# One layout change in a DRAM scratch copy: x stored by whole rows instead of by quarter rows

## The chip, the cores and the metric

The kernel runs on one core of one Trainium2 chip. The metric is the device time of one execution in microseconds (us). The kernel before was timed three times; the median is 4287.6 us. A further execution was profiled, and every view of the profile below is of that one.

## The reference, cut to what matters

The input x is 32 images of 48 channels, 64 rows (h) and 128 columns (w), in fp32: 50.3 MB. Two layers follow each other. Each layer normalises its input by groups of channels (the mean and the variance over 3 channels, 64 rows and 128 columns), sends the result through four scans, and adds the layer's unnormalised input back, which the texts below call the residual.

```python
def step(w, b):
    def f(carry, inp):
        nxt = inp + _conv1d(carry, w, b)     # 48 -> 48 channels, 5 taps
        return (nxt, nxt)
    return f
# down over h, up over h, right over w, left over w: 63, 63, 127, 127 steps
x = x + conv(_gn(x), layer 0)
x = x + conv(_gn(x), layer 1)
```

Every step of a scan needs the whole result of the step before. So the 2 x 4 scans form a long chain of small convolutions, and batches of images are the only thing that is independent.

## The kernel before, in words

**Tiles.** The images are taken in 4 groups of 8 (`GB`). A position along h or w is split into a block and a place within the block, each block 8 long (`E8`): w = 8k + e, with 16 blocks k; h = 8a + i, with 8 blocks a. One row of one group fills 3 tiles (`NG`) of 128 partitions, which hold 8 places e x 48 channels (the list `PIECES` says which partitions hold which), by 128 elements, which are 16 blocks k x 8 images b. One step of a scan (`step`, L728) is 9 products of 128x128 on TensorE (L741) into 3 PSUM tiles, and 3 additions on VectorE (L750), which write the new row or column in place. The column scans use the same tiles with the roles of h and w exchanged.

**Phases.** Twelve phases follow each other (`PHASES`). They are named by their number k from 0: 0 rows of group 0 in layer 0; 1 rows of group 1; 2 columns of groups 0 and 1 together; 3 rows of group 2; 4 rows of group 0 in layer 1; 5 rows of group 3 (layer 0); 6 columns of groups 2 and 3 in layer 0; 7, 8, 9 rows of groups 1, 2, 3 in layer 1; 10 and 11 the columns of layer 1. A row phase has 126 steps, a column phase 254. The names of the PSUM tiles in the profile carry this: `step_11d` is layer 1, group 1, scan down, so phase 7; `step_01l` is layer 0, pair 1, scan left, so the end of phase 6.

**Data between phases.** Three arrays in DRAM carry it. `xin` (`source[0]`) holds x in the order of the tiles, `ups` (`upa`, `upb`) the result of the row phases, and `mid` (`source[1]`) the input of layer 1.

- x is read in its own order (`take_in`, L553), permuted in SBUF by `permute` (L560, copies at L569) and written to `xin` by `put_out` (L571). `permute` makes four copies for a row r, one for each quarter q of 4 blocks k. Each copy writes 256 elements in one contiguous run (the order is e, k, b) and reads them with the image innermost, so with a step of 8 KB in the first group and 2 KB later. One call treats row h = r of the upper half of the image and h = 32 + r of the lower half, on 96 partitions (48 channels x 2 halves).
- The order of `xin` before, `mid` and `ups` is, for each channel: i, q, a, e, then 32 elements (4 blocks k x 8 images). A row read (`by_row`, used by `move_rows`, L589) so meets runs of 32 elements, 128 bytes. A column read (`by_col`) for one quarter q meets a x e x 32 elements in one run, 8 KB.
- `move_rows` moves rows between DRAM and the slots in SBUF, in pieces of 8 rows and 10 DMAs. All go to SP's queue.
- `load_residual` (L663) reads the residual of one unit (128 partitions x 2048 elements, 1 MB; a column phase has 24 units, 4 quarters j x 6) from `source[layer]` by `by_col`. In layer 0 it goes to SP's queue, in layer 1 to ACT's. `add_residual` (L670, on GpSimd, at L673) adds it, and `keep_result` (L675) writes the unit to `mid`, on SP's queue.

**What sets the order of the work.** The function `in_order` chains what each engine and each queue gets in the order of an agenda; `at(t, fn, ...)` puts a piece of work on the agenda at step number t of the scans. So SP's queue is one fixed list of DMAs. In a column phase with the left scan from step `left`, unit u is added at about left + 34 + 32 per quarter + 4.5 per unit; four staging tiles hold the residuals, and the load of unit u is issued 3 steps after the addition of unit u - 4. The rows of the following row phase (`plan_rows`, L853) are read 16 at a time at 28 and 12 steps before the phase starts, and 4 and 20 steps after it, and scaled by ACT (`scale_rows`, L606, the ACTIVATEs at L614) 13 steps before and 3, 19, 35 steps after. The steps are positions in the lists: an engine or queue that is late delays all that stands behind.

**The first group** (`first_group`, L1024) has its own list, since nothing covers it. x of group 0 is read in two halves of 16 + 16 rows r; VectorE takes its statistics (L422); rows h = 0 to 7 come straight from products with a 0/1 matrix (L1074); the others are permuted, put out to `xin`, and read back 8 rows at a time by `move_rows`, and scaled. Permuted rows pass through a ring of spare SBUF areas (`free`, `late`, `later`), so an area is written again only after its put-out has landed.

Of the kernel before, what the change touches and what calls it, by code (L numbers as in the profile page):

```python
# [42 lines left out]
GB = 8  # L43
E8 = 8
FULL = 128
NG = E8 * C // FULL
NQ = 4
# [73 lines left out]
def kernel(  # L121
# [8 lines left out]
    nc = tc.nc  # L130
    B, _, H, W = x.shape
    NK = W // E8
    NH = H // E8
    KQ = NK // NQ
    WQ = W // NQ
    N = NK * GB
    RUN = KQ * GB
    LINE = E8 * RUN
# [75 lines left out]
    def by_row(t, e, h0, h1):  # L214


        t = t.rearrange("c (i q a e n) -> e a c i q n", i=E8, q=NQ, a=NH, e=E8)[e, h0 // E8]
        return t[:, h0 % E8 : h0 % E8 + h1 - h0].rearrange("c i q n -> c (i q) n")

    def lines(t, h0, h1):  # L220

        t = t.rearrange("c (i q a n) -> a c i q n", i=E8, q=NQ, a=NH)[h0 // E8]
        return t[:, h0 % E8 : h0 % E8 + h1 - h0].rearrange("c i q n -> c (i q) n")

    def by_col(t, e, j):


        return t.rearrange("c (i q n) -> i q c n", i=E8, q=NQ)[e, j]

    def dma(dst, src, queue=None):  # L230
        (queue or nc.sync).dma_start(dst, src)
# [21 lines left out]
    def pieces(o):  # L253
        return [(e, c0, c1, p0) for e, c0, c1, g, p0 in PIECES if g == o]
# [22 lines left out]
    def sided(t):  # L277

        return t.rearrange("(c s) n -> s c n", s=2)
# [280 lines left out]
    def permute(nat, r0, perm, engines):  # L560

        rows = perm.shape[-1] // (W * GB)
        src = nat.rearrange("p b (r q k e) -> p r q e k b", q=NQ, k=KQ, e=E8)
        dst = perm.rearrange("p (r q e k b) -> p r q e k b", r=rows, q=NQ, e=E8, b=GB)
        for i in range(rows * NQ):
            r, q = divmod(i, NQ)
            eng = engines[i * len(engines) // (rows * NQ)]
            copy = eng.copy if eng is nc.scalar else eng.tensor_copy
            copy(dst[:, r, q], src[:, r0 + r, q])  # L569

    def put_out(g, r, perm):  # L571


        n = perm.shape[-1] // (W * GB)
        for s in range(2):
            h = s * HALF + r
            dma(
                lines(source[0][g], h, h + n),
                sided(perm)[s].rearrange("p (m n) -> p m n", n=LINE),
            )  # L580


    def row_views(k):
        return [slot[i].rearrange("p (o h n) -> p o h n", o=NG, h=HALF) for i in slots(k)]
# [4 lines left out]
    def move_rows(k, h0, h1, to_dram):  # L589

        _, layer, g = PHASES[k]
        view = row_views(k)[h0 // HALF]
        t = (ups if to_dram else source)[layer][g]
        for h in range(h0, h1, E8):
            end = min(h1, h + E8)
            for o in range(NG):
                for e, c0, c1, p0 in pieces(o):
                    here = view[p0 : p0 + c1 - c0, o, h % HALF : h % HALF + end - h]
                    here = here.rearrange("p h (q n) -> p (h q) n", q=NQ)
                    there = by_row(t, e, h, end)[c0:c1]  # L600
                    if to_dram:
                        dma(there, here)
                    else:
                        dma(here, there)
# [58 lines left out]
    def load_residual(k, j, i, nat):  # L663
        _, layer, pair = PHASES[k]
        o, half = UNITS[i]
        t = source[layer][2 * pair + half]
        for e, c0, c1, p0 in pieces(o):
            dma(nat[p0 : p0 + c1 - c0], by_col(t, e, j)[c0:c1], nc.scalar if layer else None)

    def add_residual(k, j, i, nat, eng=nc.gpsimd):  # L670
        o, half = UNITS[i]
# [161 lines left out]
    def plan_input(g, times, work, lag, nats, perms):  # L833

        stats = InputStats(f"x{g}", 0)
        rows = nats[0].shape[-1] // W
        ahead, pieces_of = len(nats), rows * W // BN
        per = rows * W * GB // perms[0].shape[-1]
        for j, t in enumerate(times):
            nat = nats[j % ahead]  # L840
            if j == 0 and g > 1:
                at(t - 7, take_in, g, 0, nat)
            for i in range(per):
                perm, r = perms[i % len(perms)], i * rows // per
                at(t + i * work / per, permute, nat, r, perm, [nc.gpsimd])
                at(t + i * work / per + 4, put_out, g, rows * j + r, perm)
            at(t + lag, stats.take_others, pieces_of * j, nat)
            if j + ahead < len(times):
                free = t + 7
                at(free, take_in, g, rows * (j + ahead), nat)  # L850
        spread(t + work + lag + (0, 2, 32, 5)[g], scaling(f"x{g}", 0, g, stats, x_masks, (0, 0, 8, 0)[g]), 1)

    def plan_rows(k, t0, prev):  # L853
        if k == 1:
            ahead, scaled = (-34, -18, -3, 12), (-12, -2, 17, 33)
        elif prev == "cols":
            ahead, scaled = (-28, -12, 4, 20), (-13, 3, 19, 35)
        else:
            ahead, scaled = (-54, -43, 0, 11), (-22, -8, 16, 30)
        if k:  # L860
            for i in range(4):
                at(t0 + ahead[i], move_rows, k, i * LOAD, (i + 1) * LOAD, False)
                at(t0 + scaled[i], scale_rows, k, i * LOAD, (i + 1) * LOAD)

        cuts = list(range(0, H + 1, E8))
        following = PHASES[k + 1][0] == "cols"
        if following and follows(k + 1):
            cuts = [0, E8 // 4] + cuts[1:]
        for h0, h1 in zip(cuts, cuts[1:]):
            t = t0 + 2 * (H - 1) - h0  # L870
            if k == 0:
                t += 16 if h0 >= HALF else 68
            elif not following:
                t = t0 + 92 + 5 * (H - h1) / E8 + (34 if h1 <= HALF else 0)
            at(t, move_rows, k, h0, h1, True)
        at(
            t0 + H - 1,
            nc.gpsimd.tensor_copy,
            last.rearrange("p (o n) -> p o n", o=NG),
            row(k, H - 1),  # L880
        )
# [6 lines left out]
    def plan_cols(k, t0, prev):  # L888
# [46 lines left out]
        for u, (t, j, i) in enumerate(direct):  # L935
            nat = tiles[u % n]
            o, half = UNITS[i]
            if u < n:
                at(left + 16, load_residual, k, j, i, nat)
            if layer == 0:  # L940
                if u >= n:
                    at(direct[u - n][0] + 3, load_residual, k, j, i, nat)
                at(t, add_residual, k, j, i, nat)
                at(t + 4, keep_result, k, j, i)
                unit = quarter(k, j)[:, half, o]
                if half == 0:
                    for b in range(GB):
                        at(t + 5 + b, stats[0].take, j, o, unit, b)
                else:
                    at(t + 1, stats[1].take, j, o, unit)  # L950
            else:

                at(t, add_residual, k, j, i, nat)
                at(t + 2.5, permute_unit, k, j, i, nat, (nc.gpsimd, nc.scalar, nc.scalar))
                if final or j not in HELD:
                    at(t + 4.5, store_result, k, j, i, nat)
                else:
                    at(t + 4.5, hold_result, j, i, nat)
                if final and j == 1:
                    at(t + 4.7, load_residual, k, 0, i, last_tiles(k)[i])  # L960

                if u >= 2 and u - 2 + n < len(direct):
                    at(t + 4.6, load_residual, k, *direct[u - 2 + n][1:], tiles[(u - 2) % n])
# [60 lines left out]
    def first_group():  # L1024
# [35 lines left out]
        def permute_rows(i, r0, r1, ring, *engines):  # L1060
            for r in range(r0, r1):
                permute(parts[i], r, ring[r % len(ring)], engines)

        def put_rows(i, r0, r1, ring):
            for r in range(r0, r1):
                put_out(0, i * rows + r, ring[r % len(ring)])
# [38 lines left out]
        for b in range(GB):  # L1105
            stats.take(NBN // 2, parts[1], b)
            stats.aggregate(b)
        move_rows(0, 8, 16, False)
        for r in range(0, 8, 2):
            permute_rows(1, r, r + 2, free, nc.gpsimd)  # L1110
# [98 lines left out]
```

## Time and profile before

| | us |
|---|---|
| three timed runs | 4284.73, 4287.6, 4297.19 |
| median | 4287.6 |
| profiled execution | 4290.3 |
| its span in the profile | 4288.2 |
| TensorE products busy in the span | 4058.9 |
| first step of phase 0 starts at | 107.8 |
| phase 3 starts, ends | 1167.3, 1427.1 |
| phase 7 starts, ends | 2442.1, 2705.3 |
| last step ends | 4207.7 |

The page gives busy time by engine, busy tenths in 40 slices (107.2 us each), the DMA queues and the costliest groups of instructions. Further views come from the same trace: stretches of time with the busy time of each engine in each (with the granted TensorE clock, the busy share of the 16 DMA engines and GB/s), timelines of one engine or queue, and lists of who waited for whom. In a group's line, `arena<-xin` means that the tile `arena` is written from `xin`. `arena` and `early` are the two large SBUF tiles, which hold the slots, the staging tiles and the spare areas. A row scan without a wait takes 124.4 us for its 63 steps (from 1679.9 to 1804.2 in the first scan of phase 5), so 1.97 us a step.

### The profile page before, as it was taken

What the parts mean: (1) busy time and instruction counts of PE and PEld (TensorE: products, weight loads), DVE (VectorE), ACT (ScalarE), POOL (GpSimd) and SP (SyncE); (2) the same over time, 40 slices, a digit from 0 to 9 for tenths busy, and PEclk for the clock granted to TensorE, in tenths of its full rate; (3) what the DMA queues carried; (4) which work ended last, traced back from release to release, by engine and by line L of the source; (5) the groups of instructions that cost most, each with busy time, mean ns of one, the idle gap of its engine ahead of it and who ended that gap; (6) DMA issues with size and microseconds to landing.
All of it is one profiled execution on the core that took longest, in us unless ns stands there. A gap on an engine that the chain in (4) does not pass through costs nothing. (4 is left out here: it accounts for less than half of the span.)

```text
span 4288.2 us, 89979 instructions
## 1 busy us (share of the span) xinstructions
PE 4058.9 (95%) x36648; PEld 4029.3 (94%) x36648; DVE 2164.5 (50%) x6503; ACT 1340.1 (31%) x2662; POOL 886.2 (21%) x906
## 2 busy tenths in 40 slices
PE   3699998999999999998999999999999999999992
PEld 1699998999999999998999999999999999999992
DVE  6345444446664444444446654444444444444443
ACT  1584301435793564100006772613000002210122
POOL 4271001325323020010005310000000024510352
PEclk9899999999999999999999999999999999999996
DMA  9599799857998979679308979939289049999999
GB/s 213 113 216 162 105 167 168 245 127 213 230 198 156 163 140 160 103 127 206 85 1 242 222 154 149 148 50 161 43 140 200 1 78 247 247 243 156 180 202 182
DMA packets 2116733, 680.12 MB, mean 159 GB/s; under 512 B 2005440, under 2 KB 2056160, under 8 KB 2076384
## 3 DMA queue, kind: packets, MB, share of 16 engines
q1 hardware_dynamic: 2015904, 581.64, 70.2%
q10 hardware_dynamic: 97216, 86.44, 9.9%
q0 software_dynamic: 3200, 6.30, 0.5%
q8 instruction: 288, 4.72, 0.5%
q14 instruction: 125, 1.02, 0.1%
HBM read 397.38 MB, written 295.98 MB: 162 GB/s over the span
## 5 line engine op out<-in xcount | busy, mean ns | idle before, releaser
L614 ACT ACTIVATE arena<-arena,offset,scale 128x256 f32<-128x256 f32 (+2 forms) x816 | 575.6, 801 | 432.9 <-DMA arena<-mid 176.1
L673 POOL TENSOR_TENSOR arena<-arena 128x2048 f32<-128x2048 f32 x80 | 363.1, 4553 | 1386.0 <-PE step_10l L741 434.1
L569 POOL COPY arena<-arena 96x256 f32<-96x256 f32 x448 | 265.0, 650 | 553.8 <-DMA arena<-in_x 444.2
L512 ACT ACTIVATE early<-arena 128x256 f32<-128x256 f32 x192 | 129.4, 674 | 477.2 <-POOL arena L673 471.2
L741 PE MATMUL step_00r<-arena,early 128*128 128x128 f32 x2286 | 251.5, 274 | 14.1 <-DMA arena<-upa 14.1
L741 PEld LDWEIGHTS step_00r<-arena,early 128*128 128x128 f32 x2286 | 251.1, 185 | 14.5 <-issue 14.4
L741 PE MATMUL step_01r<-arena,early 128*128 128x128 f32 x2286 | 250.6, 273 | 14.4 <-DMA arena<-upa 14.4
L741 PEld LDWEIGHTS step_01r<-arena,early 128*128 128x128 f32 x2286 | 250.4, 185 | 14.6 <-issue 14.5
L741 PE MATMUL step_11r<-arena,early 128*128 128x128 f32 x2286 | 251.3, 273 | 8.2 <-DVE arena L750 8.2
L741 PEld LDWEIGHTS step_11r<-arena,early 128*128 128x128 f32 x2286 | 250.8, 185 | 8.7 <-DVE arena L750 8.6
L741 PE MATMUL step_00l<-arena,wleft 128*128 128x128 f32 x2286 | 249.1, 272 | 0.0
L741 PEld LDWEIGHTS step_00l<-arena,wleft 128*128 128x128 f32 x2286 | 248.6, 184 | 0.0
L741 PE MATMUL step_10l<-arena,wleft 128*128 128x128 f32 x2286 | 248.5, 272 | 0.0
L741 PE MATMUL step_11l<-arena,wleft 128*128 128x128 f32 x2286 | 248.5, 272 | 0.0
L741 PE MATMUL step_01l<-arena,wleft 128*128 128x128 f32 x2286 | 248.4, 272 | 0.0
L741 PE MATMUL step_10r<-arena,early 128*128 128x128 f32 x2286 | 248.4, 272 | 0.0
L741 PEld LDWEIGHTS step_10l<-arena,wleft 128*128 128x128 f32 x2286 | 248.4, 184 | 0.0
L741 PEld LDWEIGHTS step_11l<-arena,wleft 128*128 128x128 f32 x2286 | 248.4, 184 | 0.0
L741 PEld LDWEIGHTS step_01l<-arena,wleft 128*128 128x128 f32 x2286 | 248.4, 184 | 0.0
L741 PEld LDWEIGHTS step_10r<-arena,early 128*128 128x128 f32 x2286 | 248.4, 184 | 0.0
L698 ACT COPY arena<-arena 128x256 f32<-128x256 f32 x172 | 99.7, 656 | 411.5 <-POOL arena L673 162.2
L240 ACT COPY early<-arena 128x1 f32<-128x1 f32 x2 | 0.4, 191 | 657.9 <-DVE arena L750 657.9
(189 smaller groups left out, 7171.3 us busy)
## 6 DMA issues: line engine op xcount, KB each, us to landing
arena<-in_x SPq DMA_DIRECT2D x24, 1536.0 KB, 11.6
xin<-arena SPq DMA_DIRECT2D x96, 384.0 KB, 4.7
arena<-xin SPq DMA_DIRECT2D x96, 384.0 KB, 8.5
mid<-arena SPq DMA_DIRECT2D x96, 384.0 KB, 7.8
arena<-mid SPq DMA_DIRECT2D x192, 192.0 KB, 4.2
upb<-arena SPq DMA_DIRECT2D x192, 192.0 KB, 3.9
arena<-upb SPq DMA_DIRECT2D x96, 384.0 KB, 12.3
arena<-xin SPq DMA_DIRECT2D x186, 192.0 KB, 4.3
```

The costliest lines, as they stand in the source:

```text
L240: fn(*args)
L512: nc.scalar.activation(junk[:, 0:n], view[:, b], AF.Identity, accum_out=self.sum[:, i, j : j + 1])
L569: copy(dst[:, r, q], src[:, r0 + r, q])
L614: nc.scalar.activation(args[0], args[0], AF.Identity, bias=args[2], scale=args[1])
L673: eng.tensor_tensor(unit, unit, nat, ALU.add)
L698: copy(by_w(perm)[:, a], src[:, a])
L741: nc.tensor.matmul(part(whole(ps[o])[0:m], -s), weights[:, i, at : at + m], part(src(i), s), start=seen[o] == 1, stop=seen[o] == left[o],)
```

## The change

`xin` alone gets another order: for each channel i, a, e and then 128 elements, which are all 16 blocks k of w x 8 images. `mid` and `ups` keep theirs. Row reads of layer 0 so meet runs of 512 bytes (`x_by_row`), the residual of layer 0 meets runs of 128 bytes, 64 for each partition and unit (`x_by_col`), and `put_out` writes 4 KB runs where it wrote 1 KB runs. `permute` makes one copy of 1024 elements for a row, or two of 512 (images 0 to 3 on GpSimd, 4 to 7 on ACT) where two engines share it in the first group. The new copies have the access 8 images x 16 blocks x 8 places: they read w in contiguous runs and write single elements with a step of 512 bytes. The count of DMAs, of products and of VectorE's operations stays, as does the order in which all of them stand.

```diff
+    def x_by_row(t, e, h0, h1):
+        t = t.rearrange("c (i a e n) -> e a c i n", i=E8, a=NH, e=E8)[e, h0 // E8]
+        return t[:, h0 % E8 : h0 % E8 + h1 - h0]
+
+    def x_by_col(t, e, j):
+        return t.rearrange("c (i m q n) -> i q c m n", i=E8, m=NH * E8, q=NQ)[e, j]
...
     def lines(t, h0, h1):
-        t = t.rearrange("c (i q a n) -> a c i q n", i=E8, q=NQ, a=NH)[h0 // E8]
-        return t[:, h0 % E8 : h0 % E8 + h1 - h0].rearrange("c i q n -> c (i q) n")
+        t = t.rearrange("c (i a n) -> a c i n", i=E8, a=NH)[h0 // E8]
+        return t[:, h0 % E8 : h0 % E8 + h1 - h0]
...
     def permute(nat, r0, perm, engines):
         rows = perm.shape[-1] // (W * GB)
-        src = nat.rearrange("p b (r q k e) -> p r q e k b", q=NQ, k=KQ, e=E8)
-        dst = perm.rearrange("p (r q e k b) -> p r q e k b", r=rows, q=NQ, e=E8, b=GB)
-        for i in range(rows * NQ):
-            r, q = divmod(i, NQ)
-            eng = engines[i * len(engines) // (rows * NQ)]
-            copy = eng.copy if eng is nc.scalar else eng.tensor_copy
-            copy(dst[:, r, q], src[:, r0 + r, q])
+        src = nat.rearrange("p b (r k e) -> p r b k e", k=NK, e=E8)
+        dst = perm.rearrange("p (r e k b) -> p r b k e", r=rows, e=E8, b=GB)
+        n = GB // len(engines)
+        for r in range(rows):
+            for i, eng in enumerate(engines):
+                copy = eng.copy if eng is nc.scalar else eng.tensor_copy
+                some = slice(i * n, (i + 1) * n)
+                copy(dst[:, r, some], src[:, r0 + r, some])
...
-                    there = by_row(t, e, h, end)[c0:c1]
+                    if to_dram or layer:
+                        here = here.rearrange("p h (q n) -> p (h q) n", q=NQ)
+                        there = by_row(t, e, h, end)[c0:c1]
+                    else:
+                        there = x_by_row(t, e, h, end)[c0:c1]
...
-            dma(nat[p0 : p0 + c1 - c0], by_col(t, e, j)[c0:c1], nc.scalar if layer else None)
+            here = nat[p0 : p0 + c1 - c0]
+            if layer:
+                dma(here, by_col(t, e, j)[c0:c1], nc.scalar)
+            else:
+                dma(here.rearrange("p (m n) -> p m n", n=RUN), x_by_col(t, e, j)[c0:c1])
```

More of the change, by code (lines that the diff above doesn't have):

```diff
@@ L578, in put_out @@
                 lines(source[0][g], h, h + n),
-                sided(perm)[s].rearrange("p (m n) -> p m n", n=LINE),
+                sided(perm)[s].rearrange("p (m n) -> p m n", m=n),
             )
@@ L598, in move_rows @@
                     here = view[p0 : p0 + c1 - c0, o, h % HALF : h % HALF + end - h]
-                    here = here.rearrange("p h (q n) -> p (h q) n", q=NQ)
-                    there = by_row(t, e, h, end)[c0:c1]
+                    if to_dram or layer:
[3 more added lines that the diff above has]
+                        there = x_by_row(t, e, h, end)[c0:c1]
                     if to_dram:
```

## The prediction

> **What bounds the kernel now.** I began with the page: busy times, then the 40 slices, then the DMA queues.
>
> ```profile
> PE 4058.9 (95%) x36648; PEld 4029.3 (94%) x36648; DVE 2164.5 (50%) x6503; ACT 1340.1 (31%) x2662; POOL 886.2 (21%) x906
> ...
> DMA  9599799857998979679308979939289049999999
> ...
> q1 hardware_dynamic: 2015904, 581.64, 70.2%
> ```
>
> TensorE (PE) is busy in 95% of the span, and the change neither adds nor removes a product. So only the other 5% can shrink, and it grows wherever data comes too late. The DMA engines are full in many slices, and one queue, q1, carries most: it is SP's. The list of PE's waits says where the 5% lies.
>
> ```profile
> PE rows L1074 <- DMA arena<-in_x: 41.7, 1, 41.7
> PE step_00d L741 <- DVE arena L750: 31.7, 6, 14.9
> PE step_00d L741 <- DVE arena L625: 24.7, 1, 24.7
> PE step_01r L741 <- DMA arena<-upa: 14.4, 1, 14.4
> ```
>
> The columns are the total, the count and the longest, in us. The change touches the first group (24.7, and most of 31.7, which are waits for rows of `xin`); the read of x (41.7) and the start of the column phases (14.4 each) stay. Then I asked whether the later phases have slack: stretches of 20 us around the start of phase 7 (PE, PEld, DVE, ACT, POOL busy, PE clock, DMA share, GB/s).
>
> ```profile
> 2280.00:2300.00 20.00, 20.00 (x186) 20.00 (x186) 14.86 (x41) 19.12 (x51) 3.53 (x1) 1.00 1.02 298
> 2300.00:2320.00 20.00, 20.00 (x187) 20.00 (x186) 14.85 (x40) 6.66 (x16) 1.06 (x1) 1.00 0.68 244
> 2320.00:2340.00 20.00, 20.00 (x187) 20.00 (x186) 12.06 (x36) 11.57 (x29) 20.00 (x5) 1.00 0.79 238
> ...
> 2500.00:2520.00 20.00, 18.98 (x173) 18.78 (x172) 10.92 (x32) 19.49 (x43) 6.86 (x4) 1.00 1.05 186
> 2520.00:2540.00 20.00, 18.48 (x169) 18.29 (x167) 11.16 (x32) 15.16 (x21) 0.00 (x0) 1.00 1.05 213
> ```
>
> With 8-KB runs a full stretch moves 298 GB/s (first line); with 128-byte row reads in it, 186. From 2340 the share stays at 0.98 or more until 2540, and in the last two stretches PE itself loses time. SP's queue and PE show why.
>
> ```profile
> 2460.64 25.98 SPq L231 DMA_DIRECT2D arena<-mid  x20
> 2486.73 2.78 SPq L231 DMA_DIRECT2D arena<-xin  x3
> 2489.55 1.82 SPq L231 DMA_DIRECT2D mid<-arena  x3
> 2491.47 3.95 SPq L231 DMA_DIRECT2D arena<-xin  x3
> 2495.47 1.35 SPq L231 DMA_DIRECT2D mid<-arena  x3
> 2497.51 26.07 SPq L231 DMA_DIRECT2D arena<-mid  x20
> ```
> ```profile
> 2506.87 31.61 PE L741 MATMUL step_11d<-arena,early 128*128 128x128 f32 x286 [1.02 <-issue]
> 2541.74 0.80 PE L741 MATMUL step_11d<-arena,early 128*128 128x128 f32 x2 [3.26 <-DVE arena L750]
> ```
>
> The last two row reads of phase 7 (`arena<-mid`, x20) stand in SP's queue behind residual loads of layer 0 (`arena<-xin`, 3 DMAs a unit). ACT scales those rows until 2542.8, and PE waits 3.26 us for it (the bracket). So phase 7 has **no slack** behind exactly the loads that the change makes slower.
>
> **Part 1, the residual of layer 0 (8 KB to 128-byte runs).** A unit is 1.05 MB. At 298 GB/s it takes 3.5 us. The nearest rows with 128-byte runs are whole reads of 32 rows, 6.29 MB each: 39.88 us in phase 0 (`arena<-xin x40` at 185.32) and 40.45 us (`arena<-mid x40` at 2574.96), thus 158 and 155 GB/s. At 155 a unit takes 6.8 us, 3.3 more. No row shows 128-byte runs that lie 512 bytes apart, so the bounds are 3.5 and 6.8. I take 6.8: size and engines are the same, and packets of 128 bytes have a median of 13 ns whatever they move.
>
> Into phase 7: 20 of the 24 units (all but the four staged first) lie ahead of the last row read, 20 x 3.3 = 66 us. The DMA engines idle for 6.4 + 4.2 us in the two stretches with 0.68 and 0.79; waits in the queue's order keep some of that, and I credit 9. Behind the units stand row reads, ACT's scaling and PE, all without slack: **+57**.
>
> Into phase 3 the same 66 are ahead, but here the rows come from `xin` as well and gain (part 2): four reads of 16 rows save 8.5 each, 34. The engines idle some 17 us in 985 to 1048, and ACT is about 4 us ahead of PE in the scaling (L614 ends 1263.25). 66 - 34 - 17 - 4 = **+11**.
>
> **Part 2, row reads (128 to 512-byte runs).** Packets of 448 bytes have a median of 25 ns, of 576 bytes 29; so 512 should be about 27, 0.053 ns a byte against 13 / 128 = 0.102. Sixteen rows, 3.15 MB, took about 20 us and should take about 11.5 (an estimate from these rows; the bounds are 20 and, at 298 GB/s, 10.6). Phases 1 and 5 have rows of layer 0 too. In phase 1 PE waits 0.87 + 0.98 us for rows: **-2**. Phase 5 has no wait to win.
>
> [...]
>
> **Part 3, the writes of `put_out` (1 KB to 4 KB runs).** Packets of 1,024 bytes have a median of 46 ns, of 4,096 bytes 194; times 16 engines that is 356 and 338 GB/s. The bounds are these two, so nothing.
>
> **Part 4, the copies and the first group.** Four copies of 256 elements become one of 1024. In the first group one of the old took 577 ns (the groups by form), 2.31 us a row; over the whole run 650.
>
> ```profile
> L569 POOL COPY arena<-arena 96x256 f32<-96x256 f32 x448 | 265.0, 650 | 553.8 <-DMA arena<-in_x 444.2
> ```
>
> Later groups have cover: GpSimd is busy 21% of the span. In the first group the rows of phase 0 hang on it. GpSimd's contiguous copy of 384 elements (L240) took 509 ns, 1.33 ns an element, so 1.36 us a row; on ACT a copy with a step (L512, 256 elements, 674 ns) costs over twice as much an element as a contiguous one (L443, 512 in 631 ns). The new copy has a contiguous read and a strided write; the bounds are 1.25 and, twice the old, 4.6 us a row. I take 1.6, near the contiguous row, as the strided side is now the write alone: on ACT, L614 (strided on both sides) is only a quarter above L512 (strided in its read).
>
> [...]
>
> I replayed phase 0 by hand with the wait lists of the built programs. Two things meet. First, with the new writes GpSimd's copies of rows 12 to 14 wait until put-outs of rows 8 to 11 have landed (about 69.5, behind the reads of x), though they use other areas; they ran at 48 to 64. GpSimd so pauses where VectorE works out the coefficients, which ended only when GpSimd's run of copies did (105.60):
>
> ```profile
> 83.58 22.07 DVE L389 TENSOR_TENSOR dev_x<-var_x,std_x 128x24 f32<-128x24 f32 x1
> ```
>
> This operation on 24 elements takes 0.2 us when alone, so PE starts at about 87 rather than 107.8. Second, the supply of rows still sets the end: two put-outs wait for ACT's scaling of rows 16 to 31 as before (SP stands idle from 106 to 140.84), and 14 row copies lie on the path. The last stall of phase 0, for rows from 32 on, ended at 208.6. By the replay it ends at 202 with copies of 2.31 us, at 190 with 1.25: 11.3 us for each us a row. With 1.6 it ends at 194: **-14**.
>
> **Sum.** -14 - 2 + 11 + 57 = +52. The profiled execution took 4290.3 (span 4288.2), thus 4342; it lies 2.7 above the median of the three runs, so the forecast is **4340 us**.
>
> **Rivals.**
> *Row reads gain nothing.* If 512-byte runs move no faster than 128-byte ones, phase 3 pays 66 - 17 - 4 = 45, phase 1 gains nothing, and the first group perhaps 8: -8 + 45 + 57 = +94, **4382**. For it: SP's stretches with row reads also hold writes and other reads, so their rate is not the packets' alone. Against: 27 ns between the rows of 448 and 576 bytes.
> *Slow copies.* At 4.6 us a row the first group loses 19 instead of gaining 14: +85, **4373**. The new waits for put-outs could do the same. Against it: a write with a step costs ACT only a quarter.
> *Only the full stretch counts.* If the early units are absorbed (they are issued steps ahead and the queue has time until 2372), only the 8 units between the row reads of phase 7 count, 8 x 3.3 = 26, and phase 3 pays nothing: -14 - 2 + 26 = +10, **4298**. Against it: 1.02 and 0.98 from 2340 on.
> *Other side, faster.* The residual's 128-byte runs lie in one 16-KB neighbourhood and come near the price of 8-KB runs. Then phases 3 and 7 pay nothing and -16 remains: **4272**. It decides where a unit costs under about 4.75 us (220 GB/s): 20 x 1.25 - 9 = 16 cancels the gain. Against it: 13 ns for 128 bytes in every direction, near packets or far.
>
> **How the numbers follow.** Chances: forecast 0.50 (its own range 4320 to 4365), no gain of row reads 0.12, slow copies 0.10, only the full stretch 0.16, other side 0.12. The range 4295 to 4390 takes in all but the other side and the tails. About 0.3%, 13 us, is what a measurement of this kernel can tell from no change. Faster by more: 0.11 (most of the last rival). Within: 0.09 (half of the third and a little of the last). Slower: 0.80.
>
> **What would show it.** In the new profile: unit loads (`arena<-xin`, x3) with some 6.8 us of full engines each; PE waits in `step_11d` of 29, 17 and 13 us at rows 16, 32 and 48, and about 11 us in `step_02d`; GpSimd's copy 96x1024 near 1.6 us; the first `step_00d` near 87 and the last long wait of phase 0 ending near 194; packets of 512 bytes near 27 ns. The forecast fails if units land as fast as before, if PE's stalls in phase 7 stay below 30 us, or if phase 0 ends later than 399.6.

## The result and the profile after

| | before | after |
|---|---|---|
| runs | 4 | 4 |
| median, us | 4290.7 | 4450.87 |
| lowest to highest | 4284.73 to 4297.19 | 4438.65 to 4455.89 |
| span of the profiled execution | 4288.2 | 4454.1 |

The ratio is 1.0369, with a 95% interval of 1.0342 to 1.0396: the kernel became 3.7% slower, 160 us. The forecast was 4340 us, and the range ended at 4390.

The page of the changed kernel, its busy times, DMA slices and largest queue:

```profile
PE 4077.9 (92%) x36648; PEld 4045.6 (91%) x36648; DVE 2152.5 (48%) x6503; ACT 1338.1 (30%) x2655; POOL 839.2 (19%) x536
...
DMA  6577788969997979658708997948559229989999
...
q1 hardware_dynamic: 2080416, 581.64, 71.1%
```

PE does the same 36648 products in 92% of a longer span. Its busy time grew by 19 us as well. In the stretch from 2600 below, where PE stands for 13 of 20 us, the granted clock is 0.54 and 37 products take 6.98 us; in the prediction's stretch from 2300, at a clock of 1.00, 187 took 20.00. GpSimd (POOL) has 370 instructions fewer and 47 us less work, and that bought nothing. PE's waits for the listed tiles (total, count, longest):

```profile
PE step_00d L758 <- DVE arena L638: 34.3, 1, 34.3
PE step_00d L758 <- DVE arena L767: 34.3, 5, 20.0
PE step_01d L758 <- ACT arena L627: 26.8, 2, 26.2
PE step_01l L758 <- DVE arena L767: 20.5, 1, 20.5
PE step_11d L758 <- DVE arena L767: 18.6, 1, 18.6
PE step_02d L758 <- DVE arena L767: 17.2, 2, 16.1
PE step_11d L758 <- issue: 16.0, 4, 13.9
PE step_00l L758 <- DVE arena L767: 15.4, 1, 15.4
...
PE step_02d L758 <- issue: 10.8, 4, 8.3
...
PE step_11d L758 <- DMA mid<-arena: 7.6, 1, 7.6
```

In the kernel before, phase 1 had this line:

```profile
PE step_01d L741 <- ACT arena L614: 1.8, 2, 1.0
```

Three families are to be seen: the first group (`step_00d`), phase 1 (`step_01d`), and the two transitions from a column phase to a row phase, each with waits at the end of the left scan (`step_00l`, `step_01l`, which had none) and in the row scan behind it (`step_02d`, `step_11d`). The ends of the scans give the sizes; the column "row_puts" and the next are two of the experiments below.

| end of | before | after | later by | row_puts | row_puts_long |
|---|---|---|---|---|---|
| phase 0 | 399.9 | 420.4 | 20.5 | 403.7 | 399.4 |
| phase 1 | 651.2 | 698.5 | 47.3 | 652.7 | 648.4 |
| phase 2 | 1167.4 | 1232.8 | 65.4 | 1185.8 | 1165.5 |
| phase 3 | 1427.4 | 1524.6 | 97.2 | 1476.1 | 1420.2 |
| phase 5 | 1929.0 | 2026.5 | 97.5 | 1976.2 | 1920.4 |
| phase 6 | 2442.2 | 2562.0 | 119.8 | 2513.3 | 2434.4 |
| phase 7 | 2705.6 | 2867.9 | 162.3 | 2816.7 | 2695.3 |
| last step | 4207.7 | 4370.6 | 162.9 | 4321.5 | 4197.4 |

So the loss is 47 us in phases 0 and 1, 50 around phase 3 and 65 around phase 7; the row phases without a transition, and phases 8 to 11, lose nothing.

**Where phases 0 and 1 lost.** GpSimd's timeline in the kernel before, while it permutes group 1 beside phase 0 (start, length, count of copies, and in brackets the wait ahead of them):

```profile
262.71 4.79 POOL L569 COPY arena<-arena 96x256 f32<-96x256 f32 x8 [0.90 <-DMA xin<-arena]
267.66 4.74 POOL L569 COPY arena<-arena 96x256 f32<-96x256 f32 x8 [0.16 <-DMA xin<-arena]
277.20 9.51 POOL L569 COPY arena<-arena 96x256 f32<-96x256 f32 x16 [4.79 <-DMA xin<-arena]
...
287.23 9.49 POOL L569 COPY arena<-arena 96x256 f32<-96x256 f32 x16
```

The same in the changed kernel:

```profile
272.01 3.96 POOL L579 COPY arena<-arena 96x1024 f32<-96x1024 f32 x2 [5.01 <-DMA xin<-arena]
281.01 3.97 POOL L579 COPY arena<-arena 96x1024 f32<-96x1024 f32 x2 [5.05 <-DMA xin<-arena]
290.94 3.95 POOL L579 COPY arena<-arena 96x1024 f32<-96x1024 f32 x2 [5.96 <-DMA xin<-arena]
```

Two rows take 4.0 us of copying instead of 4.8, but each pair is now followed by about 5 us or more of waiting for a put-out. GpSimd is done with group 1 at 402.5 rather than 351.0, and phase 1 waits for its rows. It was not the price of the copies that grew but the waits between them. Why, the wait lists of the built programs show: the put-out of the first staging tile waits for the copies into the second tile as well (before, for its own rows alone), so copies and put-outs no longer overlap. The trace agrees: a pair of copies ends at 275.97, its put-outs begin at 275.99 and land at 280.87, and the next copy begins at 281.01; in the kernel before, a put-out began at 257.14 with copies running on until 261.81.

**Where the transitions lost.** Two stretches of the changed kernel (PE, PEld, DVE, ACT, POOL busy, PE clock, DMA share, GB/s), one in phase 3 and one in phase 7:

```profile
1300.00:1320.00 20.00, 16.27 (x149) 16.08 (x147) 10.50 (x29) 12.50 (x17) 3.17 (x1) 1.00 1.13 187
2600.00:2620.00 20.00, 6.98 (x37) 6.72 (x38) 2.62 (x8) 19.72 (x37) 4.54 (x1) 0.54 1.36 160
```

The DMA engines are full, at 160 to 187 GB/s, and PE stands idle for 3.7 and 13.0 of the 20 us. SP's queue, behind one of the row reads for phase 7, shows what fills them:

```profile
2512.93 22.81 SPq L240 DMA_DIRECT2D arena<-mid  x20
2535.84 5.64 SPq L240 DMA_DIRECT2D arena<-xin  x3
2541.52 3.69 SPq L240 DMA_DIRECT2D mid<-arena  x3
2545.32 6.33 SPq L240 DMA_DIRECT2D arena<-xin  x3
2551.69 3.92 SPq L240 DMA_DIRECT2D mid<-arena  x3
2555.70 6.39 SPq L240 DMA_DIRECT2D arena<-xin  x3
```

A residual unit (`arena<-xin`, x3) takes 5.6 to 6.4 us of the queue, where it took 2.78 to 3.95 before (the prediction's lines at 2486.73 and 2491.47). From the start of a left scan to the end of the next scan down, the packets of the trace add up (the sum of the packets' times over 16 engines; packets overlap, up to 32 are under way at once, so these sums are not time of the clock):

```
                        all     128-byte packets          512-byte packets
kernel        window, us  us    MB      us   mean ns      MB      us   mean ns
before          377.9   320.4   12.58   94.7  15.4        -
after           430.3   417.8   25.17  207.0  16.8        12.58   74.0  48.2
row_puts_long   376.5   295.2   -                         12.58   69.6  45.3
before_short    447.3   416.8   37.75  278.8  15.1        -
```

In the kernel before, the 12.58 MB are the rows of phase 3; after, they are the 512-byte packets, and the 25.17 MB are the residual's 24 units.

### The profile page after: what moved, and what is told of

Its sections match the earlier page's. It is cut to its first block, busy times and chain, and to the rows that moved or that the text cites. A ratio compares the mean times of both kernels' runs of the same rounds, so it can differ in the third digit from the quotient of the medians.

```text
span 4454.1 us, 89587 instructions
## 1 busy us (share of the span) xinstructions
PE 4077.9 (92%) x36648; PEld 4045.6 (91%) x36648; DVE 2152.5 (48%) x6503; ACT 1338.1 (30%) x2655; POOL 839.2 (19%) x536
## 5 line engine op out<-in xcount | busy, mean ns | idle before, releaser
L579 POOL COPY arena<-arena 96x1024 f32<-96x1024 f32 (+1 forms) x115 | 221.0, 2020 | 676.7 <-DMA arena<-in_x 415.9
L758 PE MATMUL step_01l<-arena,wleft 128*128 128x128 f32 x2286 | 250.4, 273 | 20.5 <-DVE arena L767 20.5
L758 PE MATMUL step_00l<-arena,wleft 128*128 128x128 f32 x2286 | 252.3, 274 | 15.4 <-DVE arena L767 15.4
L758 PE MATMUL step_00r<-arena,early 128*128 128x128 f32 x2286 | 250.8, 273 | 14.3 <-DMA arena<-upa 14.3
L758 PE MATMUL step_01r<-arena,early 128*128 128x128 f32 x2286 | 250.9, 273 | 13.9 <-DMA arena<-upa 13.9
L452 ACT ACTIVATE early<-arena 96x512 f32<-96x512 f32 x192 | 121.1, 631 | 264.4 <-DMA arena<-in_x 198.8
```

Of the source, the lines that this page charges most:

```text
L452: nc.scalar.activation(junk[0:PX], piece, AF.Identity, accum_out=self.sum[:, at[0], at[1]],)
L579: copy(dst[:, r, some], src[:, r0 + r, some])
L758: nc.tensor.matmul(part(whole(ps[o])[0:m], -s), weights[:, i, at : at + m], part(src(i), s), start=seen[o] == 1, stop=seen[o] == left[o],)
```

## The experiments

The number behind each name is the median; ratios are to the kernel before, run on the same chip, with their 95% intervals. "After" stands for the changed kernel.

**split_access.** The accesses in SBUF are cut as before (a copy takes 2 of the 8 places e, 256 contiguous elements); layout and runs stay as after.

```diff
-        src = nat.rearrange("p b (r k e) -> p r b k e", k=NK, e=E8)
-        dst = perm.rearrange("p (r e k b) -> p r b k e", r=rows, e=E8, b=GB)
+        src = nat.rearrange("p b (r k e) -> p r e k b", k=NK, e=E8)
+        dst = perm.rearrange("p (r e k b) -> p r e k b", r=rows, e=E8, b=GB)
+        n = E8 // NQ
+        for i in range(rows * NQ):
+            r, q = divmod(i, NQ)
...
+            some = slice(q * n, (q + 1) * n)
+            copy(dst[:, r, some], src[:, r0 + r, some])
...
-                sided(perm)[s].rearrange("p (m n) -> p m n", m=n),
+                sided(perm)[s].rearrange("p (m q n) -> p m q n", m=n, q=NQ),
```

> The new layout and the new runs stay; only the accesses in SBUF are cut as before: four copies of 256 elements a row, contiguous in the write, and put-outs that name four pieces of 256 elements. In the built program the waits of GpSimd, SP and VectorE in phase 0 are then those of the kernel before. Theory W (the accesses of 1024 elements bring waits for other areas, and these cost what phases 0 and 1 lost, 47 us at the end of phase 1): first step_00d back to about 108, phase 1 ends near 651, total 4451 - 47 = 4404, give or take 8. Rival C (the loss of phases 0 and 1 comes from slower row reads or put-outs of the new layout): within 10 of 4451.

Measured: 4457.29 us, ratio 1.0372 (1.0355 to 1.039). Theory W fell as it was put: it was right for the scan down of phase 0 and wrong for what follows. That scan ended at 272.4 (273.0 before, 285.5 after), but the scan up behind it lost 12 us, so that phase 0 ended at 411.6, and phase 1 still ended 40.5 us late. GpSimd again copied two rows and waited 5 us. The wait lists then showed that the put-outs of two rows (groups 1 to 3; the first group has one row each) still waited for the copies of the other tile.

**row_puts.** As split_access, and each put-out of two rows becomes two of one row.

```diff
+            for i in range(n):
+                h = s * HALF + r + i
+                row = sided(perm)[s][:, i * W * GB : (i + 1) * W * GB]
+                dma(lines(source[0][g], h, h + 1), row.rearrange("p (m q n) -> p m q n", m=1, q=NQ))
```

> As split_access, but a put-out of two rows becomes two put-outs of one row, each naming four pieces of 256 elements. In split_access phase 0 was back to its old end and the loss sat in groups 1 and later: there a put-out of two rows waited for the copies into the other staging tile (GpSimd copied 5 us, then waited 5 us, and so on). In the built program of this kernel each put-out waits for its own row's copies alone. Theory W2: the 41 us at the end of phase 1 go, 4457 - 41 = 4416, give or take 8; phase 1 starts near 400 and step_01d waits under 5 us. Rival C: the copies and row reads themselves are late, step_01d still waits over 15 us, 4440 or more.

Measured: 4402.8 us, ratio 1.0244 (1.0227 to 1.0262). W2 holds: phase 1 ends at 652.7, and `step_01d` has no wait over 0.5 us left. GpSimd's timeline beside phase 0:

```profile
273.44 9.51 POOL L581 COPY arena<-arena 96x256 f32<-96x256 f32 x16 [5.19 <-DMA xin<-arena]
...
283.62 9.51 POOL L581 COPY arena<-arena 96x256 f32<-96x256 f32 x16 [0.22 <-POOL early L250]
```

Copies of four rows follow each other again, although they cost 2.4 us a row where the copies of 1024 elements cost 2.0.

**whole_copies.** The changed kernel's copies with the put-outs of row_puts: the other half of the same split.

```diff
-                sided(perm)[s].rearrange("p (m n) -> p m n", m=n),
+                    row.rearrange("p (m q n) -> p m q n", m=1, q=NQ),
```

> The changed kernel's copies of 1024 elements with the one-row, four-piece put-outs of row_puts. In the built program VectorE's first scaling waits for no put-out any more, but put-outs still wait for the copies of the rows beside them, and copies for the put-outs beside them. If it is these waits that cost phase 1 (W2), phase 1 still starts 30 to 45 us late and the total is 4440 to 4450, with the first step_00d near 87 to 90. If the form of the put-outs alone matters, it is like row_puts, about 4416.

Measured: 4452.33 us, ratio 1.0363 (1.0348 to 1.0379). PE begins at 86.4, and phase 1 ends 46.7 us late all the same. With split_access and row_puts this makes the split complete: the waits between copies and put-outs go only when both accesses are small. Here PE also starts where the prediction said, with the changed kernel's copies. It gained nothing: `step_00d` waits 62.3 us for VectorE's additions inside phase 0, where after it waits 34.3 ahead of it and 34.3 inside.

**res_long, split_long, row_puts_long.** The residual's runs are 8 KB again, in after, in split_access and in row_puts.

```diff
-                dma(here.rearrange("p (m n) -> p m n", n=RUN), x_by_col(t, e, j)[c0:c1])
+                dma(here, by_col(t, e, j)[c0:c1])
```

> The changed kernel, but the residual of layer 0 is read in 8-KB runs from the same places in memory, so it adds other elements of x: read for its time. Theory R (the residual's 128-byte runs are the whole loss of both transitions, 18 + 32 in the left scan of phase 2 and phase 3, 22 + 43 in phase 6 and phase 7, the stalls in the left scans included): 4451 - 115 = 4336, phases 3 and 7 with at most 5 us of waits. Rival L (the stalls of the left scans and part of phase 3 come from the late put-outs and the 512-byte reads): 4385 to 4400, with the left scans still stalled.

> Both edits: accesses cut in four, and the residual in 8-KB runs (other elements of x are added: read for its time). What is left of the change is the 512-byte row reads alone. Theories W and R together: 4451 - 47 - 115 = 4289; if the 512-byte row reads are worth what their packets save (21 us of 16 engines for a phase), 4275 to 4289. If W or R is not the whole, what stays above 4291 is the unexplained part.

> As row_puts, with the residual read in 8-KB runs (other elements of x are added: read for its time). Now only the 512-byte row reads and the 4-KB writes are left of the change. W2 and R together: 4331 - 41 = 4290, equal to the kernel before within 10. If the 512-byte reads were worth what the prediction gave them (8.5 us for 16 rows, 14 us in the first group), 4270 to 4280.

Measured: 4331.35 us, 1.0076 (1.0061 to 1.0091); 4331.46 us, 1.0081 (1.0061 to 1.0101); 4283.76 us, 0.9967 (0.9956 to 0.9979). The 120 us between the medians of after and res_long (126 by the ratios, as the two stood beside different runs of the kernel before), and the 119 us between row_puts and row_puts_long, are the residual's runs. The waits of the left scans go with them, so Rival L fell: by the ends of the scans, res_long is 44.7 us late after phase 1, and from there to the end of phase 3 it takes 2.8 us less than the kernel before, through phases 6 and 7 0.4 more. What is then left of the change, 512-byte row reads and 4-KB writes, gains 0.33%, 14 us (12 by the medians). PE's waits in row_puts_long, the longest:

```profile
PE rows L1095 <- DMA arena<-in_x: 41.9, 1, 41.9
PE step_00d L762 <- DVE arena L771: 28.3, 6, 13.7
PE step_00d L762 <- DVE arena L642: 27.6, 1, 27.6
PE step_00r L762 <- DMA arena<-upa: 14.9, 1, 14.9
PE step_01r L762 <- DMA arena<-upa: 14.6, 1, 14.6
PE step_11r L762 <- DVE arena L771: 8.5, 1, 8.5
```

Neither transition has a line here.

**before_short.** The other way round: the kernel before, with the residual in 128-byte runs and nothing else.

```diff
+                dma(here.rearrange("p (m n) -> p m n", n=RUN), x_by_col(t, e, j)[c0:c1])
```

> The kernel before, with only the residual of layer 0 read in 128-byte runs 512 bytes apart (other elements of x are added: read for its time). Theory R: a unit costs 8.6 us of all engines rather than 3.7, 24 units 118 us, so phases 2 and 3 lose the 50 of the changed kernel plus about 15 (the rows keep their 128-byte runs), phases 6 and 7 lose 65: 4291 + 130 = 4421. Rival L: phase 3 loses less than 20 without the 512-byte reads, 4291 + 65 + 20 = 4376 or less. With the 6.8 us a unit of the prediction: 66 - 17 - 4 = 45 and 57, 4393.

Measured: 4432.57 us, ratio 1.031 (1.0294 to 1.0325), 133 us. One edit makes most of the loss, about as much as theory R said (130). By the ends of the scans it loses 67.3 us into phase 3 and 69.4 into phase 7. By packets' times its 24 units take 278.8 - 94.7 = 184 us, 7.7 a unit.

**before_short12.** Only the 12 units that are done before the row reads begin have 128-byte runs.

```diff
+            elif j < 2:
+                dma(here, by_col(t, e, j)[c0:c1])
```

> As before_short, but only the first 12 of the 24 units (the quarters j = 3 and 2) are read in 128-byte runs (other elements of x are added: read for its time). They are done with before the row reads of the next phase begin. Theory D (the sum of the engines' time counts): half of the extra 4 us x 24, thus 48 us of engines for a transition, less the idle time there: 20 to 50 us in all, 4318 to 4348. The third rival of the prediction (only the units between the row reads count): within 8 of the kernel before, about 4298.

Measured: 4339.73 us, ratio 1.0109 (1.0083 to 1.0136): 46 us. PE waits in the row scans, long after these units:

```profile
PE step_11d L751 <- DVE arena L760: 10.2, 1, 10.2
PE step_02d L751 <- DMA arena<-xin: 9.4, 1, 9.4
```

The third rival of the prediction, that only the units in the full stretch count, is refuted: the early units cost PE 25.9 us into phase 3 and 21.0 into phase 7.

**no_stats.** VectorE's statistics stand behind the addition of the residual and ahead of the scan's own additions. Here they are left out.

```diff
-                    for b in range(GB):
-                        at(t + 5 + b, stats[0].take, j, o, unit, b)
+                    if u == 0:
+                        at(t, nc.vector.memset, stats[0].st, 1.0)
```

> The changed kernel, but VectorE takes no statistics of layer 1 for the even groups (their tile is filled with ones: read for its time). These 8 operations a unit stand in VectorE's queue behind GpSimd's addition of the residual and ahead of the scan's own additions. Theory H (they turn a late residual into PE stalls, and these are a loss of their own): the waits of step_00l and step_01l (15 and 21 us) go and the total falls by 30 to 45, to 4405 to 4420. Rival D (the DMA engines are the limit, the stall is only taken earlier): the two waits go, phases 3 and 7 wait by as much longer, total within 10 of 4451.

Measured: 4450.94 us, ratio 1.0362 (1.0345 to 1.0379), the same time as after. PE's waits:

```profile
PE step_11d L758 <- DVE arena L767: 49.2, 6, 25.4
...
PE step_02d L758 <- DVE arena L767: 31.9, 6, 20.4
```

The waits of the left scans are gone (15.4 and 20.5 us) and have come back in the row scans. So Rival D holds. Here the head of VectorE's queue decided where PE waits (the left scans or the row scans), and not how long: the time stayed within 0.1 us of after.

**row_puts_act.** The residual of layer 0 goes to ACT's queue.

```diff
-                dma(here.rearrange("p (m n) -> p m n", n=RUN), x_by_col(t, e, j)[c0:c1])
+                dma(here.rearrange("p (m n) -> p m n", n=RUN), x_by_col(t, e, j)[c0:c1], nc.scalar)
```

> As row_puts, with the residual of layer 0 loaded from ACT's queue instead of SP's, so that the row reads of phases 3 and 7 no longer stand behind it in one queue. Theory D (all 16 engines are full of 128-byte packets, whichever queue they come from): the left scans and the row scans still lose about 115 us together, 4403 give or take 12. Rival Q (the order in SP's queue is what delays the rows): the waits of step_02d and step_11d shrink by half or more, 4350 to 4375.

Measured: 4541.06 us, ratio 1.0578 (1.0552 to 1.0605). Neither theory said this: the left scans now wait 58.7 and 45.0 us. The run doesn't tell D from Q, since ACT also scales the rows and takes half of the statistics, and now issues loads in between. Which of these held it up was not separated.

**before_near, rows_near_long.** Are packets dear because they lie far apart?

```diff
+                there = t.rearrange("c (i h m r n) -> i h r c m n", i=E8, h=2, r=2, n=RUN)
+                dma(here.rearrange("p (m n) -> p m n", n=RUN), there[e, j // 2, j % 2][c0:c1])
...
+                        there = t.rearrange("c (i a f s n) -> i a s c f n", i=E8, a=NH // 2, s=2, n=N)
+                        there = there[e, a // 2, a % 2][c0:c1, i0 : i0 + end - h]
```

> As before_short, but the 128-byte runs of a unit lie 256 bytes apart instead of 512 (other elements of x are added: read for its time). Theory P (each packet has its price, near or far): within 8 of before_short, 4433 less what the chip differs. Rival N (the distance sets the price): 15 us or more below before_short, with a mean packet under 14 ns in the left scans instead of 15.1.

> As row_puts_long, but the 512-byte runs of a row read of groups 2 and 3 lie 1 KB apart instead of 32 KB (other rows are read: read for its packets). In row_puts_long a 512-byte packet takes 45 ns in the mean where the prediction had 27. Theory N2 (the 32-KB steps between the runs are the reason): near 27 to 32 ns in phases 3 and 5. Theory P2 (512 bytes into one partition cost this much when all engines read): 43 to 48 ns again.

Measured: 4417.95 us, ratio 1.029 (1.0267 to 1.0312), an interval that overlaps that of before_short, with 16.6 ns for a 128-byte packet instead of 15.1; and, in the one run of rows_near_long (4285.37 us), 43.6 ns for a 512-byte packet in phase 3 against 45.3. Distance is not the reason in either, between 256 and 512 bytes and between 1 KB and 32 KB.

**before_pause, row_puts_pause, row_puts_long_pause.** In row_puts_act PE began at 89.3 and phase 2 15 us earlier than in row_puts, with the same instructions up to there: VectorE's operation at 84.3 took 0.28 us, not 22, by luck of the moment at which it met GpSimd's copies, as I read it. Here GpSimd is made to pause at that place.

```diff
         for r in range(0, 8, 2):
+            if r == 4:
+                for _ in scaling("x0", 0, 0, stats, x_masks):
+                    pass
+                hold = stat_pool.tile([FULL, NG, GB], F32, tag="hold", name="hold")
+                nc.gpsimd.tensor_copy(hold, coeffs[0, 0][1])
             permute_rows(1, r, r + 2, free, nc.gpsimd)
             put_rows(1, r, r + 2, free)
-        for _ in scaling("x0", 0, 0, stats, x_masks):
-            pass
```

> The kernel before, with one small copy on GpSimd (24 elements of the new coefficients into a tile of its own) between the copies of the second half's rows 0 to 3 and 4 to 7 of the first group, so that GpSimd waits there until VectorE has the coefficients. Theory V (the 22 us are a stand-still of VectorE beside GpSimd's unbroken copies, and phase 0 can use about 13 of them, as in row_puts_act): first step_00d near 88, phase 2 starts 10 to 15 us earlier, total 12 us under the kernel before. Rival S (the supply of rows sets the end of phase 0, as in whole_copies): PE starts near 88 and waits as much longer for rows, total within 4 of before.

> row_puts with the same small copy. Theory V: 4403 - 13 = 4390. Rival S: 4403 within 4.

> row_puts_long (the residual in 8-KB runs adds other elements of x: read for its time) with the same small copy. Theory V: 4284 - 13 = 4271. Rival S: 4284 within 4.

Measured: 4288.35 us, 0.9978 (0.9969 to 0.9987); 4394.19 us, 1.0228 (1.0214 to 1.0243); 4274.88 us, 0.9949 (0.9934 to 0.9963). The times are 7 to 9 us lower than without the pause, between the two theories. Only before_pause ran beside its kernel without the pause; for the other two the intervals with and without overlap. In before_pause, GpSimd and then VectorE:

```profile
75.04 6.95 POOL L569 COPY arena<-arena 96x256 f32<-96x256 f32 x12
87.28 0.46 POOL L1114 COPY hold<-offset 128x24 f32<-128x24 f32 x1 [5.29 <-DVE offset L401]
87.69 7.87 POOL L569 COPY arena<-arena 96x256 f32<-96x256 f32 x9
```
```profile
85.63 0.29 DVE L387 RECIPROCAL std_x<-std_x 128x24 f32<-128x24 f32 x1
85.96 0.18 DVE L389 TENSOR_TENSOR dev_x<-var_x,std_x 128x24 f32<-128x24 f32 x1
```

GpSimd gives up 5.29 us, the operation takes 0.18 us rather than 22.07, and PE starts at 88.8 rather than 107.8. Of these 19 us phase 0 keeps 4.1, phase 1 another 2.3: the supply of rows takes the rest. before_pause keeps the old layout, leaves nothing of the computation out, and is faster than both kernels, by 0.2% against the kernel before.

## Why the prediction was wrong, point by point

The direction was right, and its largest term held: into phase 7 +57 was forecast, and 65 came, from the cause that was named. The sum was +52 and became +162. Three things carry the miss: the waits of the copies and put-outs in phases 0 and 1 (points 1 and 2), the gain of the row reads (point 4) and the idle time of the DMA engines (point 5). The prediction's own sign of failure came as well: phase 0 ended at 420.4, later than 399.6.

| term | forecast | measured | what the runs show |
|---|---|---|---|
| first group | -14 | +20.5 | waits between copies and put-outs |
| phase 1 | -2 | +26.8 | the same waits, in group 1 |
| into phase 3 | +11 | +50 | row reads gain less, idle time not gained |
| into phase 7 | +57 | +65 | idle time not gained |

1. **"Later groups have cover: GpSimd is busy 21% of the span."** This is the step that failed worst. A busy share is no cover for a chain in which each link waits for another queue. Group 1 must be in `xin` when phase 1 begins, and its copies and put-outs take turns. I had read the new waits out of the built program for the first group, and did not read on into group 1. It cost 26.8 us there, and row_puts takes it back.

2. **"PE starts at about 87 rather than 107.8."** I listed the new waits of GpSimd and of the put-outs, and missed the one on VectorE: its first scaling waits for put-outs of the areas beside its rows. The changed kernel's timeline has it:

```profile
116.28 0.56 DVE L638 TENSOR_TENSOR arena<-arena,scale 128x384 f32<-128x384 f32 x1 [29.88 <-DMA xin<-arena]
```

   So PE began at 119.0. In whole_copies this wait is gone and PE did begin at 86.4, but phase 0 ended no earlier. The replay of the rows failed with it: the last long wait of phase 0 was to end at 194 and ended at 221.9, later than the 208.6 of the kernel before. The gain of a pause, taken alone, is 7 to 9 us (the three pause runs). The whole of the waits in phases 0 and 1 is the step from after to row_puts, 1.0369 to 1.0244, 54 us by the ratios and 48 by the medians; the rival "slow copies" mentioned them in half a sentence and gave them 19.

3. **The price of a unit: 6.8 us, 3.3 more than with 8-KB runs.** This held for what PE lost. 20 units at 3.3 are 66 us, and before_short lost 67.3 and 69.4; in before_short12 the 12 short units less the 4 staged first make 8 x 3.3 = 26 us, and it lost 25.9 and 21.0. The reason given beside it, a median of 13 ns a packet, carried nothing: the median is 13 before and after, while the mean is 15.4 before and 16.8 after (in the transition). By packets' times a unit takes 207.0 / 24 = 8.6 us, against about 3.7 for 8-KB runs, but these times overlap. By the same sum the two reads of 32 rows that gave 6.8 (39.88 and 40.45 us, with almost nothing beside them) have mean packets of 14.6 and 14.3 ns, 7.5 and 7.3 us a unit.

4. **Row reads: 8.5 us saved in 16 rows.** In SP's queue, which is where the prediction's 20 us were read, the 32 rows of phase 0 took 28.27 us instead of 39.88:

```profile
200.72 28.27 SPq L240 DMA_DIRECT2D arena<-xin  x40
```

   That is 5.8 us saved in 16 rows. By packets' times in the transition it is 94.7 / 4 - 74.0 / 4 = 5.2. Four reads so gain 21 to 23 instead of 34, and PE shows 20: before_short, with 128-byte row reads, lost 67.3 us into phase 3, row_puts 47.3. Nor were the 11.5 us what their own rows give: 20 x 0.053 / 0.102 is 10.4. Of the 512-byte packets in the transition one in eight takes 27 ns or less; the mean is 48.2 there and 48.7 in the read above. The rival "row reads gain nothing" was too low and the forecast too high. The 11.5 us after 20 would have been 42% off; the runs show 29% off in SP's queue and 22% by packets' times (18.5 us after 23.7).

5. **The idle time: 17 + 4 us credited into phase 3, 9 into phase 7.** None of it shows in the result: the 66 us of point 3 are reached without a credit, and 66 less the 20 of the row reads is 46 into phase 3, where row_puts lost 47.3 and after 49.9. Counted from the packets, the time with no packet under way did fall: from the start of the left scan to the end of the next scan down it was 57 us before and 40 after on the way into phase 3, 81 and 75 on the way into phase 7. But the whole time that the engines were short of 16 packets hardly moved (82 and 76 us, 119 and 125), as more of it passed with a few packets under way. The runs fix the net loss of a unit, not its parts: a higher price with some of it covered would look the same. One figure was also misread: from 985 to 1048 the view gives a DMA share of 0.83, 10.7 us of idle time rather than 17.

6. **The copies: 1.6 us a row.** They took 2.0 to 2.2 in the groups by form (2071 ns into `arena`), nearer to the 2.31 of the four old copies than to the 1.36 of my row of contiguous copies; no run here shows why. It moved nothing: GpSimd's waits, not its copies, were late.

What held: next to nothing in the writes of `put_out` (into phase 3, by packets' times, 3.00 MB in 1-KB packets took 10.8 us before, 3.15 MB in 4-KB packets 10.5 after); no slack in phase 7; the waits of `step_11d` at rows 16, 32 and 48 (18.6, 13.9 and 7.6 us for 29, 17 and 13, with 20.5 already taken in the left scan, which I had not placed there); no loss in the phases without a transition. The rival "other side" had a unit's runs within 16 KB; 64 runs 512 bytes apart span 32 KB, and before_near, at 16.6 ns a packet against 15.1, shows that nearer runs are no cheaper.

By the medians the steps from the kernel before to the changed one are these (they are differences of one chain of runs, so that they add up by construction, and the last one crosses runs made beside different runs of the kernel before): 4296.2 (before, in the runs of row_puts) - 12.4 for the row reads with the copies and put-outs as before, + 119.0 for the residual, + 48.1 for the waits between copies and put-outs = 4450.9.

What stays open: why an access of 1024 elements in the program brings waits for areas beside it (that it does, the wait lists and row_puts show; the rule behind it was not looked for); why 512-byte packets take 48 ns in the mean where one in eight takes 27 or less; how a unit's loss divides into price and cover; and what held up ACT in row_puts_act.

## What to carry to other kernels

Before an edit off the critical path is costed at nothing, follow its waits in the built program through every stage that issues it, not only the first: here fewer and larger copies and put-outs lost 48 us by waits alone, at a lower busy time. Credit no idle time of the DMA engines to work that stands in a queue of fixed order until a run shows it: without the credit the prediction's price gives 66 us for a transition, and before_short lost 67 and 69. Set the layout by the side that is on the path: short runs for the residual cost 119 us, long runs for the rows gave 12 to 14. A wait that one takes out of an engine's queue can come back behind it when the DMA engines are full, as the 15.4 and 20.5 us of the left scans did in no_stats.

## What the runs showed of the hardware that was not expected

- A VectorE operation with two inputs in SBUF, on 24 elements, stood 22.07 us beside GpSimd's unbroken copies (some 38 of about 0.58 us), while a copy and a reciprocal just ahead of it took 0.18 and 0.29 us. In row_puts it was another operation of this kind, 28.53 us for 8 elements; in row_puts_act none, with the same instructions, and there GpSimd's 24 copies beside them took 16.80 us instead of 13.83. Nor does every such operation stand: in the kernel before, two more (L357 and L359) took 0.44 and 0.54 us at 78.80 and 79.28, beside the same copies. Why one stands and the next does not, no run here shows.
- By the time in SP's queue, 32 rows (6.29 MB) with almost nothing beside them come at 158 GB/s in 128-byte runs (39.88 us) and at 223 in 512-byte runs (28.27 us). By packets' times over 16 engines, in the transition, 128-byte reads move 133 GB/s in the kernel before (12.58 MB in 94.7 us) and 122 when more of the traffic is of their kind (25.17 MB in 207.0 us), 512-byte reads 170 to 181 (12.58 MB in 74.0 and 69.6 us). The two measures differ, and only figures of one measure can be compared.
